# A graph layer on one core: 35 packed and 14 gathered blocks for 37 and 12, with evictions on either of two engines

## The chip, the cores and the metric

The kernel runs on one core of one Trainium2 chip. The metric is the device time of one execution in microseconds (us). Five engines take part: TensorE (PE in the profile), VectorE (DVE), ScalarE (ACT), GpSimd (POOL) and SyncE (SP, which only issues DMAs).

## The reference, cut to what matters

`x` holds 6250 rows of 128 numbers; 100,000 edges go from row `src` to row `dst`, sorted by `dst`, each of one of two types.

```python
Xs = X[src]
m_data = Xs @ W_data.T + b_data
m_ctrl = Xs @ W_control.T + b_control
msg = jnp.where((edge_types == 0)[:, None], m_data, m_ctrl)
agg = jax.ops.segment_sum(msg, dst, num_segments=X.shape[0])
out = jax.nn.relu(agg + (X @ W_self.T + b_self))
x = layernorm(x + out)          # over the last axis, eps 1e-5
```

So every row receives the sum of the messages of its incoming edges, adds its own product, passes through relu, is added to `x` and normalised.

## The kernel before, in words

**The table.** A message depends only on the source row and the type, so the kernel first computes all 2 x 6250 possible messages: per block of 128 rows one fp32 matmul with the two weights (`multiply`, L453). Each result is split into three bf16 pieces whose sum is the fp32 value (`take`, `leave`), which is why a message is 384 numbers wide. The table stays in SBUF as `m3` (98 tiles of 128 rows) and is also written to HBM (`store`).

**The destinations.** The 6250 rows are 49 blocks of 128. A block's edges lie in a window of 18 x 128 edges, found from the sorted list (`starts`). Blocks are summed in one of two ways.

*Packed blocks* (the first 37, NPB). They are prepared in groups (GROUPS, L36: eight groups of 4 or 5 blocks). For a group, `edge_fields` derives each edge's table tile and row; `bucket_hots` makes one-hot tables `hot_st` (L546); `ranks` numbers the edges of each table tile with a chain of 18 steps, each a matmul with `tri` on PE, a reduction `slot` on VectorE (L563) and a matmul with `rest` on PE; `fill_a` and `fill_b` (L600) place the edges in 32 slots per tile; `fill_c` writes the slots to HBM (`packed`) and treats those that did not fit. Then, per block, SP spreads 784 KB of slots over all partitions (`rows`, L718), VectorE makes one-hots of them (L725), and the block is done in 25 steps (NS). A step selects the messages of four table tiles with four column matmuls (`gather`, "g", L754) into one of four PSUM buffers, evicts them from PSUM to bf16 (`evict`, "e", L769) into one of eight SBUF buffers, and adds them to their destinations with four more (`add_up`, "s"). The helper `by_columns` (L232) issues these four matmuls, of 32 columns each; many different sums therefore show under L232.

*Gathered blocks* (the last 12, NG). GpSimd fetches the messages of 128 edges straight from the HBM table with an indirect DMA (`gather_rows`, "msg", L854), 18 for a block, into MB = 3 buffers. One-hots of the destinations (`gathered_hots`, L866) and four column matmuls each (`gathered_sums`, "gm") add them up.

Both kinds add the block's own product (`own_of`), sum the three pieces, apply relu, add `x` and take mean and variance on VectorE (`finish_blocks`, `finish_gathered`). `normalise` works on a group, or on the GQ blocks of a gathered piece, at a time: a root on ScalarE, a few small VectorE steps, one ScalarE `apply` per block (L190), one store.

**What sets the order.** Each engine executes its instructions in the order in which the program emits them, and waits where an operand is missing. That order is written by `Order.run` (L76): every stream above yields steps with a name, a cost per allowed engine ("T", "V", "A", "G", "S" for TensorE, VectorE, ScalarE, GpSimd, SP) and the steps that it needs. The planner keeps a clock per engine, takes the step that can start first, and among those that can start within 0.1 us on that engine the one that is due first. A step that may run on two engines goes to the one where it can start sooner, ScalarE at a tie. `due` (L388) computes the due times from constants: BUILT, when the table is complete; BLOCK, the time for a packed block; PACE, the time for one gathered tile, which is also the planned cost of a gather on GpSimd; AHEAD and FIRST, how long before its first block the preparation of a group has to end.

Before the change an eviction may go to VectorE only in the last group:

```python
costs = {"A": 0.37, "V": 0.53} if b >= STARTS[-1] else {"A": 0.37}
e = yield step(("e", b, g), costs, ("g", b, g), *free)
```

Of the kernel before, what the change touches and what calls it, by code (L numbers as in the profile page):

```python
# [32 lines left out]
ES = ER // RJ  # L33
EPS = 1e-05

GROUPS = (4,)*2+(5,)*5+(4,)  # L36
Q = max(GROUPS)
NPG = len(GROUPS)
NPB = sum(GROUPS)
NG = NB - NPB  # L40
STARTS = [sum(GROUPS[:i]) for i in range(NPG)]
R = 32
# [58 lines left out]
def step(name, costs, *needs, lag=0.0):  # L101
    return as_tuple(name), costs, [as_tuple(n) for n in needs], lag
# [7 lines left out]
def kernel(  # L110
# [95 lines left out]
    with ExitStack() as main:  # L206
        sums_over_windows(main, tc, x, xt, edges, w, bias, table, packed, total,
                          add_parts, finish, load_rows, norm)
# [6 lines left out]
def sums_over_windows(ctx, tc, x, xt, edges, w, bias, table, packed, total,  # L215
                      add_parts, finish, load_rows, norm):
    nc = tc.nc
    V, A, G, T = nc.vector, nc.scalar, nc.gpsimd, nc.tensor
# [64 lines left out]
    for j in range(RJ):  # L283
# [17 lines left out]
    counted = {n: const.tile([P, P, n], BF16, name=f"count{n}")  # L301
               for n in sorted({DC, CH, *GROUPS})}
    tri = const.tile([P, P], BF16, name="tri")
# [5 lines left out]
    slot_values = [const.tile([P, (Q + 1) // 2, NT], BF16, name=f"vs{i}") for i in range(2)]  # L309
    slot_b = {n: const.tile([P, R, n], BF16, name=f"slot{n}") for n in sorted({*GROUPS})}  # L310

# [68 lines left out]
                  for g, n in enumerate(PARTS) for b in range(at_part[g], at_part[g] + n, 2)]  # L380


    LEAD, BUILT = 8.0, 78
    BLOCK = 12.9
    PACE = 2.2
    AHEAD, FIRST = 22.0, 14

    def due(kind, *i):  # L388
        if kind in ("p", "g") and i[0] in ("root", "rooted", "scale", "apply", "out"):
            n = i[1] + 1  # L390
            return BUILT + 10 + (BLOCK * sum(p[2] for p in PIECES[:n]) if kind == "p" else PACE * KT * GQ * n)
        if kind in ("counted", "turned", "first"):
# [21 lines left out]
        if kind in ("win", "xs", "agg", "o", "whole", "sum"):  # L414
            b = i[0]
            begun = BUILT + (BLOCK * b if b < NPB else PACE * KT * (b - NPB))
            if kind == "win":
                return due("fields", blocks[b][0]) - 8 if b < NPB else BUILT - 20
            if b >= NPB:
                return begun + {"whole": PACE * KT + 2, "sum": PACE * KT + 5}.get(kind, 0)  # L420
            return begun + {"whole": BLOCK + 0.5, "sum": BLOCK + 3}.get(kind, 0.3 * BLOCK)
        if kind in ("rows", "sel", "d", "g", "e", "s"):
            of = {"rows": 1, "sel": 1, "d": 2}.get(kind, NS)
            lead = {"rows": -9, "sel": -3, "d": -1, "g": 0, "e": 1, "s": 2}[kind]
            return BUILT + BLOCK * (i[0] + (i[1] / of if len(i) > 1 else 0)) + lead
        if kind in ("gh", "gm", "msg"):
            k = i[1] * CH if kind == "gh" else i[1]
            return BUILT + PACE * (i[0] * KT + k) + {"msg": 0, "gh": 2, "gm": 5}[kind]
        n = GROUPS[i[0]]
        end = BUILT + BLOCK * STARTS[i[0]] - (AHEAD if i[0] else FIRST)  # L430
        span = BLOCK * n if i[0] else 34.0
        begun = end - span
# [324 lines left out]
    def evict():  # L757
        for i, (b, g) in enumerate(tiles):
            free = [("s", *tiles[i - EB])] if i >= EB else []
            if g == NS - 1 and b:  # L760
                free.append(("s", b - 1, g))
            costs = {"A": 0.37, "V": 0.53} if b >= STARTS[-1] else {"A": 0.37}
            e = yield step(("e", b, g), costs, ("g", b, g), *free)
            if g < NS - 1:
                gs, at = late.tile([P, D3], BF16, name="gs", bufs=EB), slice(P)
            else:
                gs, at = mixed[blocks[b][0] % 2], slice(2 * R, P)
            gs_tiles[b, g] = gs
            (A.copy if e == "A" else V.tensor_copy)(gs[at], g_tiles.pop((b, g))[at, :D3])  # L769
# [62 lines left out]
    rel_g = const.tile([P, NG, KT], BF16, name="rel_g")  # L832
    msgs, g_hots, kept = {}, {}, []
    GQ = -(-NG // -(-NG // Q))
    MB, XB = 3, 2

    def gathered_fields():
        yield step("idx", {"V": 1.8}, ("y", NB * 3 // 4), *[("win", b) for b in range(NPB, NB)])
# [10 lines left out]
    def gather_rows():  # L849
        for i, (j, k) in enumerate(gathered):  # L850
            free = [("gm", *gathered[i - MB])] if i >= MB else [*stored, "idx"]
            yield step(("msg", j, k), {"G": PACE}, *free, lag=3.0 - PACE)
            msgs[j, k] = late.tile([P, D3], BF16, name="msg", bufs=MB)
# [41 lines left out]
    def close_build():  # L895
# [7 lines left out]
        load_x(), starts(), edge_fields(), ranks(), fill_c(), fill_a(), fill_b(),  # L903
        spread(), select(), finish_blocks(),
        normalise([(lambda g=g: (hs_[g], mvs[g]), STARTS[g] + q0, q0, n) for g, q0, n in PIECES], "p"), add_up(), gather(), evict(), to_hots(), bucket_hots(),
        multiply(), take(0, "yh", "y"), leave(0, "y1", "yh"),
        take(1, "ym", "y1"), leave(1, "y2", "ym"), take(2, "yl", "y2"), constants(), store(), close_build(),
# [136 lines left out]
```

## Time and profile before

| | |
|---|---|
| time, median of 3 runs | 594.62 us (592.69 to 597.58) |
| profiled execution | 628.32 us |
| its span, first to last instruction | 626.6 us |
| mean granted TensorE clock | 0.978 |
| busy: PE, DVE, ACT, POOL | 554.5, 448.2, 448.4, 255.6 us |
| selections (L754) | 3626 matmuls |
| evictions (L769) | 892 on ACT, 33 on DVE |
| gathers (L854) | 216 |
| first selection; first and last packed sum (L153) | 82.4; 101.4 and 603.3 us |
| first gather issue; last gathered sum | 87.3; 609.5 us |

The profile is one execution, and the profiler makes it longer than an undisturbed one; the place of things is read from it, and the time from the runs. In the groups, `L754 PE MATMUL g_ps<-m,rows 128*32 128x384 bf16 x3626 | 347.7, 332 | 6.2 <-issue 2.9` means: line 754, on PE, 3626 matmuls that write `g_ps`; busy for 347.7 us in all where overlaps count once, 332 ns for one; PE had been idle for 6.2 us just before them, and most of that ended without a visible releaser. In the waits, a row names who waited, for whom, the total in us, how often, and the longest. A busy share of an engine is an average over stages, so the windows (busy time of each engine in one stretch) are read beside it.

### The profile page before, as it was taken

The numbers are of one execution on the slowest core, as the hardware profiler recorded it, in microseconds if no ns is written. First come the engines' busy times: TensorE is split into PE (matmuls) and PEld (weight loads), VectorE is DVE, ScalarE is ACT, GpSimd is POOL, SyncE is SP. The second block draws the span as 40 slices with busy tenths as digits, with TensorE's granted clock in tenths as the row PEclk, the third lists the DMA queues.
The fourth block names the chain that finished last, engine by engine and source line by source line (L and its number), as shares of the span: only waits on it lengthen the run. The fifth ranks groups of instructions, "written<-read, shape, count | busy, mean of one in ns | idle before, by whom it ended". The sixth has DMA issues, their size and how long they took to land.

```text
span 626.6 us, 27468 instructions
## 1 busy us (share of the span) xinstructions
PE 554.5 (88%) x11703; PEld 453.8 (72%) x11703; DVE 448.2 (72%) x1031; ACT 448.4 (72%) x1066; POOL 255.6 (41%) x232
## 2 busy tenths in 40 slices
PE   5899879999999989899999989999998899998950
PEld 3555447887887778787887877788886788777730
DVE  4645687897888786688768876788857766568650
ACT  6756546768877767688678768778787887777631
POOL 1000025544545445545455345455435444444330
PEclk9999989999999999999999999999999999999985
DMA  3669653243434442444324433434424443533120
GB/s 106 187 170 273 203 198 111 53 157 107 136 121 149 118 116 61 153 123 133 106 61 160 125 104 110 146 121 127 129 56 155 135 123 103 158 102 119 45 58 21
DMA packets 59642, 77.37 MB, mean 123 GB/s; under 512 B 15344, under 2 KB 50395, under 8 KB 59511
## 3 DMA queue, kind: packets, MB, share of 16 engines
q1 hardware_dynamic: 47653, 50.56, 25.4%
q0 software_dynamic: 10704, 21.56, 12.5%
q10 hardware_dynamic: 1154, 3.41, 1.8%
q8 instruction: 93, 1.52, 1.0%
q14 instruction: 38, 0.31, 0.2%
HBM read 62.44 MB, written 13.07 MB: 120 GB/s over the span
## 4 chain that ended last, share of the span: by engine, by line
PE 73%; DMA 9%; DVE 5%; issue 5%; ACT 4%; POOL 1%; SPq 1%; another core or an unknown queue 0%; ACTq 0%; POOLq 0%; DVEq 0%
PE agg L232 25%; PE g_ps L754 23%; PE acc L232 8%; DMA msg<-table,idx 7%; PE agg_g L232 6%; PE small L600 5%; PE y L460 3%; ACT gs L769 2%; PE y L478 1%; POOL msg L854 1%; DVE slot L563 1%; ACT h_p L190 1%; DMA rows<-packed 1%; PE y L462 1%; DVE two L584 1%
## 5 line engine op out<-in xcount | busy, mean ns | idle before, releaser
L769 ACT CAST gs<-g_ps 128x384 bf16<-128x384 f32 x856 | 357.8, 494 | 120.8 <-PE g_ps L754 85.7
L754 PE MATMUL g_ps<-m,rows 128*32 128x384 bf16 x3626 | 347.7, 332 | 6.2 <-issue 2.9
L854 POOL DMA_INDIRECT msg<-table,idx x216 | 243.4, 1127 | 263.6 <-PE agg_g L232 122.7
L232 PE MATMUL agg<-gs,hot_d 128*32 128x384 bf16 x3552 | 321.9, 334 | 16.7 <-ACT gs L769 8.2
L232 PEld LDWEIGHTS <-hot_d 128*32 128x32 bf16 x3700 | 212.5, 137 | 47.1 <-issue 36.3
L754 PEld LDWEIGHTS <-rows 128*32 128x32 bf16 x3626 | 201.4, 138 | 31.2 <-issue 25.6
L563 DVE TENSOR_REDUCE slot<-acc 128x5 bf16<-128x490 f32 (+1 forms) x144 | 90.2, 627 | 76.2 <-PE acc L232 49.8
L232 PE MATMUL agg_g<-msg,hot_g 128*32 128x384 bf16 x864 | 93.7, 333 | 13.5 <-DMA msg<-table,idx 11.2
L739 DVE TENSOR_TENSOR hot_d<-count,to 128x1664 bf16<-128x1664 bf16 x74 | 78.7, 1066 | 10.8 <-ACT to L634 5.1
L600 PE MATMUL small<-hot_st,two 128*32 128x98 bf16 x1332 | 66.2, 283 | 2.3 <-DVE ls L684 1.5
L232 PE MATMUL acc<-hot_st,tri 128*32 128x490 bf16 (+1 forms) x576 | 65.4, 359 | 0.2 <-issue 0.2
L232 PE MATMUL acc<-hot_st,rest 128*32 128x490 bf16 (+1 forms) x544 | 60.1, 361 | 6.2 <-DVE slot L563 5.6
L232 PEld LDWEIGHTS <-hot_g 128*32 128x32 bf16 x864 | 46.0, 124 | 19.5 <-issue 18.1
L471 ACT CAST m<-y 128x512 bf16<-128x512 f32 (+1 forms) x75 | 40.9, 580 | 25.9 <-PE y L462 12.8
L600 PEld LDWEIGHTS <-two 128*32 128x32 bf16 x1332 | 53.9, 116 | 6.5 <-issue 2.9
L546 DVE TENSOR_TENSOR hot_st<-count,st_b 128x2940 bf16<-128x2940 bf16 (+1 forms) x24 | 45.0, 1880 | 13.5 <-PE small L600 9.7
L694 POOL DMA_INDIRECT mixed<-table,row_i x8 | 9.9, 1234 | 83.2 <-DVE rows L725 79.0
L725 DVE TENSOR_SCALAR rows<-rows,pid 128x3136 bf16<-128x3136 bf16 x37 | 38.6, 1042 | 2.8 <-DMA rows<-packed 2.3
L460 PE MATMUL y<-w_sb,xt 128*128 128x256 f32 x98 | 34.4, 438 | 1.8 <-DMA xt<-in_xt 1.8
L232 PEld LDWEIGHTS <-rest 128*32 128x32 bf16 x544 | 24.1, 98 | 15.1 <-issue 14.3
L153 DVE TENSOR_REDUCE whole<-agg 128x128 f32<-128x384 f32 x37 | 20.5, 553 | 11.2 <-PE agg L232 5.6
L769 DVE CAST gs<-g_ps 128x384 bf16<-128x384 f32 x32 | 17.2, 555 | 15.2 <-PE g_ps L754 14.4
(140 smaller groups left out, 440.6 us busy)
## 6 DMA issues: line engine op xcount, KB each, us to landing
rows<-packed SPq DMA_DIRECT2D x37, 784.0 KB
table<-m SPq DMA_DIRECT2D x10, 768.0 KB
msg<-table,idx POOLq DMA_INDIRECT x216
xt<-in_xt ACTq DMA_DIRECT2D x5, 512.0 KB
xt_p<-in_xt SPq DMA_DIRECT2D x37, 64.0 KB
xs_p<-in_x SPq DMA_DIRECT2D x37, 64.0 KB
out<-h_p SPq DMA_DIRECT2D x5, 320.0 KB
win<-in_edges SPq DMA_DIRECT2D x37, 27.0 KB
```

The source lines that it names most:

```text
L153: nc.vector.tensor_reduce(whole, agg.rearrange("p (i c) -> p c i", i=3), axis=AX.X, op=ALU.add)
L232: T.matmul(out[c : c + 32], lhsT[:, c : c + 32], rhs, **flags)
L460: T.matmul(y[:, j, :], xts[g][:, b + j - at_part[g], :], w_sb[:, : 2 * D], start=j == 0, stop=False, skip_group_check=True)
L471: A.copy(part_of(b, n, i), ys[b][:, :n, :].rearrange("p b (t c) -> p t b c", t=2))
L546: V.tensor_tensor(hot, counted[n][:, None, 1 : NT + 1, :].to_broadcast([P, KC, NT, n]), fields[grp][2][:, c * KC : c * KC + KC, None, :].t ...
L563: V.tensor_reduce(slots[grp][:, k, :], by_q, axis=AX.X, op=ALU.max)
L600: T.matmul(vt[c0 : c0 + R, q // 2, :], two[:, k % KC, i, :, q], hot[:, k % KC, :, q], start=k == 0 and q < 2, stop=k == KT - 1, skip_group ...
L725: V.tensor_scalar(rows[b], rows[b], pid1, None, op0=ALU.is_equal)
L739: V.tensor_tensor(hot, counted[DC][:, :, :n], places[grp][:, q, None, c * DC : c * DC + n].to_broadcast([P, P, n]), op=ALU.is_equal)
L754: T.matmul(g_ps[t * R : (t + 1) * R, :D3], rows[b][:, :, s], m3[:, s, :], start=True, stop=True)
L769: (A.copy if e == "A" else V.tensor_copy)(gs[at], g_tiles.pop((b, g))[at, :D3])
L854: G.indirect_dma_start(out=msgs[j, k], out_offset=None, in_=table[:, :], in_offset=bass.IndirectOffsetOnAxis(ap=idx[:, j, k : k + 1], axis=0),
```

## The change

Seven groups of five blocks replace the eight groups, so 35 blocks are packed and 14 gathered. The condition on the eviction is dropped, so the planner may give any eviction to VectorE. The gathers get five buffers for three and a planned pace of 1.75 us for 2.2. The other constants of the due times move with these. GQ, the number of gathered blocks that are normalised together, follows from NG and Q and becomes 5 (pieces of 5, 5 and 4) where it was 4.

```diff
-GROUPS = (4,)*2+(5,)*5+(4,)
+GROUPS = (5,)*7
...
-    LEAD, BUILT = 8.0, 78
-    BLOCK = 12.9
-    PACE = 2.2
-    AHEAD, FIRST = 22.0, 14
+    LEAD, BUILT = 8.0, 76
+    BLOCK = 13.1
+    PACE = 1.75
+    AHEAD, FIRST = 26.0, 20
...
-            costs = {"A": 0.37, "V": 0.53} if b >= STARTS[-1] else {"A": 0.37}
+            costs = {"A": 0.37, "V": 0.53} 
...
-    MB, XB = 3, 2
+    MB, XB = 5, 2
```

## The prediction

> **What bounds the kernel now.** I read the page first for the engines' shares and the slices, then the windows for one stage at a time, the timeline for how closely TensorE issues, the waits for who is late, and the groups for durations.
>
> ```profile
> span 626.6 us, 27468 instructions
> PE 554.5 (88%) x11703; PEld 453.8 (72%) x11703; DVE 448.2 (72%) x1031; ACT 448.4 (72%) x1066; POOL 255.6 (41%) x232
> PE   5899879999999989899999989999998899998950
> ```
>
> TensorE (PE) is the busiest, with nines almost throughout; VectorE (DVE) and ScalarE (ACT) follow at 72% each. By the windows:
>
> ```profile
> core 0: us, PE busy (x) PEld busy (x) DVE busy (x) ACT busy (x) POOL busy (x), PEclk, DMA share, GB/s
> 300.00:350.00 50.00, 47.35 (x1120) 41.02 (x1114) 38.67 (x82) 36.82 (x91) 24.59 (x23) 1.00 0.40 123
> 500.00:550.00 50.00, 47.72 (x1129) 40.15 (x1121) 31.89 (x76) 39.38 (x97) 22.69 (x22) 1.00 0.42 128
> ```
>
> In the steady stage PE is busy 47 of 50 us, DVE 39, ACT 37. A busy PE need not be a full one, so I look at its spacing:
>
> ```profile
> 340.94 0.39 PE L754 MATMUL g_ps<-m,rows 128*32 128x384 bf16 x4
> 341.11 0.39 PE L232 MATMUL agg_g<-msg,hot_g 128*32 128x384 bf16 x4
> 341.27 0.39 PE L232 MATMUL agg<-gs,hot_d 128*32 128x384 bf16 x4
> ```
>
> Four column matmuls start every 0.164 us although one lasts 0.33: when nothing is late, the four-matmul set is the unit of work and costs 0.164 us. The waits say how much of that is lost:
>
> ```profile
> POOL msg L854 <- PE agg_g L232: 122.7, 78, 3.8
> POOL msg L854 <- PE g_ps L754: 107.0, 96, 4.1
> ACT gs L769 <- PE g_ps L754: 85.7, 126, 7.1
> DVE slot L563 <- PE acc L232: 49.8, 43, 2.4
> PE agg_g L232 <- DMA msg<-table,idx: 11.2, 10, 2.4
> PE agg L232 <- ACT gs L769: 8.2, 15, 1.1
> ```
>
> Everybody waits for PE, hundreds of microseconds in total; PE waits for others only some tens. POOL's gathers wait for PE to free one of three buffers. So a PE instruction taken out of the steady stage should shorten it.
>
> [...] The trace has 555 and 494, and 0.51 and 0.42 apart when queued. [...] the chain shows [...] 7.71 for one that shares the engines with a 784 KB spread of rows.
>
> ```profile
> L769 ACT CAST gs<-g_ps 128x384 bf16<-128x384 f32 x856 | 357.8, 494 | 120.8 <-PE g_ps L754 85.7
> L754 PE MATMUL g_ps<-m,rows 128*32 128x384 bf16 x3626 | 347.7, 332 | 6.2 <-issue 2.9
> L854 POOL DMA_INDIRECT msg<-table,idx x216 | 243.4, 1127 | 263.6 <-PE agg_g L232 122.7
> L769 DVE CAST gs<-g_ps 128x384 bf16<-128x384 f32 x32 | 17.2, 555 | 15.2 <-PE g_ps L754 14.4
> ```
>
> **The change, part by part.** The sum is against the profiled execution, 628.3 us (span 626.6 and 1.7 around it); the median of the runs shown is 594.62, 0.946 of it, and I scale the result with that.
>
> (a) *Blocks 36 and 37 turn from packed to gathered.* PE time of a packed block: selection 98 matmuls / 4 x 0.164 = 4.02; adding 25 x 0.164 = 4.10; ranks, 35 sets per group of five at about 0.21 = 7.35 / 5 = 1.47; filling, 36 matmuls of 98 columns at 0.055 (the chain takes 0.11 for two) = 1.98; own rows 0.28; positions and list about 0.3. Sum 12.1. A gathered block: 18 x 0.164 + 0.28 = 3.2. Check: 37 x 12.1 + 12 x 3.2 = 486, less the ranking and filling of the first eight blocks (8 x 3.45 = 28, done before the first selection) = 458, in the 521 us from the first selection (82.4) to the last packed sum (603.3): 88% of the stage, consistent with windows of 47 in 50 that also hold latencies. Two blocks: 2 x 8.9 = 17.8 us of PE work; at the same 88%, **-20.2**. It all lies on the bound; bounds -17.8 (the lost 12% doesn't shrink) and -24.
>
> (b) *36 more gathers*, each one POOL issue of 1.13 us: 41 us, POOL from 41% to about 50% busy. Covered by POOL's 264 us of waiting. DVE gets two blocks of hot_g (3 x 0.55) and loses two blocks of packed work (about 10.8 from 38.6/50 x 13.94 us per block); SP loses two spreads, two loads and two pairs of own-row loads, and gets as many for the gathered list. 0 on the path.
>
> (c) *Pace 1.75 and five buffers.* Today the gathers run from 87.3 to 606.2, 2.41 us each. The due times put the last gathered matmuls at 76 + 441 + 5 = 522 in planned time, packed blocks end at 76 + 13.1 x 35 = 534.5; today it is 558 against 555. In the trace the gathered end is indeed late: last packed sum 603.3, last gathered 609.5, and four `apply` steps and a store after it.
>
> ```profile
> 609.53 0.56 DVE L153 TENSOR_REDUCE whole<-agg_g 128x128 f32<-128x384 f32 x1 [3.19 <-PE agg_g L232]
> 612.66 1.65 ACT L190 ACTIVATE h_g<-h_g,shift,rstd 128x128 f32<-128x128 f32 x4 [1.25 <-DVE shift L184]
> ```
>
> With packed blocks last, the end is the one-block piece, whose apply ended at 606.9 today, against 614.3: at most -7.4; I take **-5**, least 0 if gathers stay last. Of the 11.2 us for which PE waits for gathers, 3.8 lie in that end; a buffer's round of 5 x 1.9 against 3 x 2.4 us leaves room for the 7.71 us landing: **-3**, bounds -7 and +8 [...].
>
> (d) *Seven groups of five; FIRST, BUILT, BLOCK, AHEAD.* The first group grows by a block: DVE slot 18 x (0.664 - 0.565) = 1.8, hot_st 3 x 0.31 = 0.9, hr and two 3 x 0.3 = 0.9, before the first selection; one constant copy (0.5 on ACT) goes. **+3**, bounds 0 and +6. The four-wide tables go elsewhere at no cost. GQ goes from 4 to 5: three normalisations of gathered blocks as before. Due times only reorder.
>
> (e) *Evictions on either engine.* How many move? In the last group, where both may do it now, DVE took 33 of 100; there DVE's other work fills 17.6 of 50 us (33.7 less 16.05 of evictions), 65% free. In the steady stage 23% is free. In proportion 33% x 23/65 = 12%, **2.9 of 25 per block**; this is my estimate, bounds 0 and 6. Thirty blocks make 87, the last five 40, less 33 today: 94 more x 0.555 = +52 us on DVE, -46 on ACT. DVE in the steady stage goes from 77% to 88%. What I add is a queueing cost: DVE works in order, and an eviction may sit behind a 2 us hot_st or a slot that waits for PE, with PE's adding matmul waiting for it. If one in four holds PE for 0.25 us: 87 x 0.25 x 0.25 = **+5**; the gain from a less crowded ACT, out of the 8.2 + 2.6 us that PE waits for it, I put at 0 net of that. Bounds -8 and +25.
>
> Sum: -20.2 - 5 - 3 + 3 + 5 = **-20**: 608 profiled, x 0.946 = **576**. What is late next is DVE, not ACT.
>
> **Rivals.**
> *DVE becomes the bound (slower).* Place: the steady stage, where DVE must keep the ranks of the next group, the one-hot tables and now evictions in one order. For: DVE is already at 77% and its longest operation is 2 us. Per packed block DVE has 10.75, with the larger gathered share (0.40 for 0.32 of 2.96 us) 10.98. At k evictions it is 10.98 + 0.555 k; if DVE can be filled to 93%, 35 blocks take as long as today's 516 us at k = 4.9. From five of 25 it decides; at k = 6, 35 x 14.3 / 0.93 = 538, +22: 650 profiled, **615**. Against: the planner gives VectorE an eviction only where it is free sooner. Chance 0.20, the milder part of it above 600.
> *The gathers don't reach the pace (no change).* 252 gathers in today's 519 us need 2.07 us each; POOL alone could do 1.13 + 0.3, buffers at worst (0.95 + 7.7 + 0.4) / 5 = 1.8. If landing times stretch with density and PE stalls on them, the gain of (a) is eaten: about **593**. Chance 0.16. Against: POOL waits for PE, not the reverse.
> *ACT was holding PE more than the waits show (larger gain).* PE fills the stage to 91%: 440 / 0.91 = 484, -37 with the same end and start: **557**. Chance 0.12.
> *No eviction moves.* The closer pace and two blocks remain, without the +5: 571; part of the forecast's case.
>
> **Numbers.** Forecast (567 to 586) 0.52, larger gain 0.12, no change 0.16, slower 0.20. Range 558 to 604: it leaves out the lower part of the larger gain (0.05) and most of the slow case's upper end (0.13). The runs before spread over 0.8%, so 1% is about what can be told from no change. Faster by over 1%: 0.66; within 1%: 0.14; slower: 0.20.
>
> **What would show it.** Per packed block the distance from first to last packed sum, divided by 34, stays near 13.9 us; selections fall from 3626 to 3430 and gathers rise to 252. (c) the last gathered sum comes before the last packed sum. (e) some 130 evictions on DVE, DVE at 85 to 90% in the steady windows and PE still at 94%. It is wrong if PE's waits for DVE evictions grow to tens of microseconds or PE falls under 45 in 50 (DVE rival), or if waits for gathers grow past 20 us (pace rival).

## The result and the profile after

The changed kernel takes 549.8 us (median of 4 runs, 548.52 to 551.42) where the kernel before takes 593.65 us beside it (590.95 to 597.58): ratio 0.926, 95% interval 0.920 to 0.932. Forecast were 576 us and a range of 558 to 604, so the sign was right and the gain was more than twice the forecast: 44 us where some 19 were expected.

One thing about the profile on which the prediction stood: that execution took 628.3 us, over 5% longer than every other execution of the same kernel in that set. A second profile of the kernel before took 602.4 us (span 600.7), and after is compared with that one from here on. That the profiler as such lengthens an execution, as I had written, isn't borne out: the profiled execution of the kernel after took 550.7 us, in the middle of its four runs, and of the eleven changed versions below it was the longest run in four and the shortest in three. The first lines of the page, of the kernel after:

```profile
span 549.0 us, 26381 instructions
PE 506.4 (92%) x11222; PEld 439.9 (80%) x11222; DVE 456.9 (83%) x1027; ACT 402.5 (73%) x943; POOL 294.6 (54%) x267
PE   5899978899999999999989999989999999989991
```

and of the kernel before, profiled again:

```profile
span 600.7 us, 27468 instructions
PE 533.0 (89%) x11703; PEld 459.9 (77%) x11703; DVE 446.4 (74%) x1031; ACT 445.0 (74%) x1066; POOL 256.4 (43%) x232
PE   5899968999998998899998989979997999989950
```

PE has less to do and is idle for less of the time; VectorE and GpSimd are busier. The windows of the kernel after (columns: stretch, its length, then busy time and instruction count of PE, weight loads, DVE, ACT, POOL, granted clock, DMA share, GB/s):

```profile
300.00:350.00 50.00, 49.60 (x1205) 45.03 (x1201) 45.40 (x95) 40.25 (x99) 35.01 (x31) 1.00 0.50 148
400.00:450.00 50.00, 49.45 (x1219) 45.32 (x1216) 45.32 (x107) 40.86 (x102) 34.61 (x30) 1.00 0.52 160
```

VectorE now works 45 of 50 us, as (e) foresaw, and PE is at 49.5 all the same. The groups of the kernel after that answer to those shown of before:

```profile
L769 ACT CAST gs<-g_ps 128x384 bf16<-128x384 f32 x739 | 313.5, 491 | 92.8 <-PE g_ps L754 72.5
L854 POOL DMA_INDIRECT msg<-table,idx x252 | 284.7, 1130 | 140.3 <-PE g_ps L754 70.9
L754 PE MATMUL g_ps<-m,rows 128*32 128x384 bf16 x3430 | 315.4, 331 | 0.1
L769 DVE CAST gs<-g_ps 128x384 bf16<-128x384 f32 x101 | 54.6, 553 | 19.2 <-PE g_ps L754 14.8
```

103 evictions went to VectorE (two more write `mixed`). Where the time went, by stage, from the second profile of before to the one of after:

| | before again | after | difference |
|---|---|---|---|
| start to first selection (L754) | 81.7 | 81.4 | -0.3 |
| first selection to last packed sum (L153) | 495.6 | 456.4 | -39.2 |
| last packed sum to the end of the span | 23.4 | 11.2 | -12.2 |
| span | 600.7 | 549.0 | -51.7 |

(The two profiled executions are 52 us apart, the medians 44.) The waits of the two point to the cause of much of it; the experiments below test it. Before, profiled again (who waited, for whom: total, times, longest):

```profile
POOL msg L854 <- PE agg_g L232: 104.8, 89, 4.2
POOL msg L854 <- PE g_ps L754: 91.7, 79, 4.4
PE agg_g L232 <- DMA msg<-table,idx: 31.0, 23, 3.3
```

After:

```profile
POOL msg L854 <- PE g_ps L754: 70.9, 124, 3.5
POOL msg L854 <- PE agg_g L232: 48.7, 68, 2.8
PE agg_g L232 <- DMA msg<-table,idx: 10.8, 9, 2.0
```

So POOL waited for PE, and PE waited for what POOL had issued too late. Such a circle through a set of buffers is called a ring here, and in the chain of waits of the kernel before (start, length, what) one of its turns looks like this:

```profile
314.24 1.38 POOL msg L854
315.62 0.39 issue
...
316.23 8.28 DMA msg<-table,idx
324.51 0.04 issue
324.56 0.46 PE agg_g L232 x4
325.02 0.32 PE agg L232 x4
325.34 0.32 PE g_ps L754 x4
```

From the moment when a buffer is free until its next content is in place there pass 1.4 + 0.4 + 8.3 us and small gaps, over 10 us. Three buffers at 2.3 us a gather give about 7.

### The profile page after: what moved, and what is told of

It is laid out like the page before. It is cut to its first block, busy times and chain, and to the rows that moved or that the text cites. A ratio compares the mean times of both kernels' runs of the same rounds, so it can differ in the third digit from the quotient of the medians.

```text
span 549.0 us, 26381 instructions
## 1 busy us (share of the span) xinstructions
PE 506.4 (92%) x11222; PEld 439.9 (80%) x11222; DVE 456.9 (83%) x1027; ACT 402.5 (73%) x943; POOL 294.6 (54%) x267
## 4 chain that ended last, share of the span: by engine, by line
PE 63%; DMA 15%; DVE 11%; ACT 4%; issue 3%; POOL 1%; SPq 1%; DVEq 0%; ACTq 0%; POOLq 0%
PE agg L232 20%; PE g_ps L754 19%; DMA msg<-table,idx 8%; PE acc L232 7%; PE small L600 6%; PE agg_g L232 6%; DMA rows<-packed 3%; PE y L460 3%; ACT gs L769 2%; DVE hot_st L546 2%; DVE slot L563 2%; ACT h_p L190 1%; DMA xt_p<-in_xt 1%; PE y L478 1%; POOL msg L854 1%
## 5 line engine op out<-in xcount | busy, mean ns | idle before, releaser
L769 ACT CAST gs<-g_ps 128x384 bf16<-128x384 f32 x739 | 313.5, 491 | 92.8 <-PE g_ps L754 72.5
L854 POOL DMA_INDIRECT msg<-table,idx x252 | 284.7, 1130 | 140.3 <-PE g_ps L754 70.9
L754 PE MATMUL g_ps<-m,rows 128*32 128x384 bf16 x3430 | 315.4, 331 | 0.1
L232 PE MATMUL agg<-gs,hot_d 128*32 128x384 bf16 x3360 | 295.3, 330 | 3.8 <-DVE gs L769 1.9
L754 PEld LDWEIGHTS <-rows 128*32 128x32 bf16 x3430 | 183.6, 136 | 16.8 <-issue 10.4
L232 PEld LDWEIGHTS <-hot_d 128*32 128x32 bf16 x3500 | 184.1, 137 | 13.9 <-issue 8.9
L232 PE MATMUL agg_g<-msg,hot_g 128*32 128x384 bf16 x1008 | 106.8, 329 | 10.9 <-DMA msg<-table,idx 10.8
L563 DVE TENSOR_REDUCE slot<-acc 128x5 bf16<-128x490 f32 x126 | 83.4, 662 | 19.6 <-PE acc L232 16.5
L769 DVE CAST gs<-g_ps 128x384 bf16<-128x384 f32 x101 | 54.6, 553 | 19.2 <-PE g_ps L754 14.8
L232 PEld LDWEIGHTS <-hot_g 128*32 128x32 bf16 x1008 | 51.7, 124 | 15.1 <-issue 13.5
L232 PE MATMUL acc<-hot_st,tri 128*32 128x490 bf16 x504 | 60.0, 374 | 1.2 <-DVE hot_st L546 1.2
L232 PE MATMUL acc<-hot_st,rest 128*32 128x490 bf16 x476 | 54.2, 376 | 7.4 <-DVE slot L563 7.0
L546 DVE TENSOR_TENSOR hot_st<-count,st_b 128x2940 bf16<-128x2940 bf16 x21 | 41.7, 1991 | 3.7 <-PE small L600 2.0
L232 PEld LDWEIGHTS <-rest 128*32 128x32 bf16 x476 | 21.0, 97 | 17.4 <-issue 16.2
L232 PEld LDWEIGHTS <-tri 128*32 128x32 bf16 x504 | 21.2, 98 | 3.3 <-issue 3.0
```

The lines of the kernel that those rows point to most:

```text
L232: T.matmul(out[c : c + 32], lhsT[:, c : c + 32], rhs, **flags)
L546: V.tensor_tensor(hot, counted[n][:, None, 1 : NT + 1, :].to_broadcast([P, KC, NT, n]), fields[grp][2][:, c * KC : c * KC + KC, None, :].t ...
L563: V.tensor_reduce(slots[grp][:, k, :], by_q, axis=AX.X, op=ALU.max)
L754: T.matmul(g_ps[t * R : (t + 1) * R, :D3], rows[b][:, :, s], m3[:, s, :], start=True, stop=True)
L854: G.indirect_dma_start(out=msgs[j, k], out_offset=None, in_=table[:, :], in_offset=bass.IndirectOffsetOnAxis(ap=idx[:, j, k : k + 1], axis=0),
```

## The experiments

Three theories were tried against each other. A: ScalarE's evictions held PE, and the freedom to use VectorE is the unforeseen gain. B: the blocks, the pace and the earlier end of the gathers are the gain. C: the ring of three buffers held PE, and five buffers are most of it.

**The kernel before, once more**, without an edit:

> The kernel before once more, for a second profile. The prediction took the 521 us from first selection to last packed sum as normal and read 88% of PE work in it. If that one execution was long by chance (628 us against 595), this one shows a stage of about 488 us and PE filled to about 94%, and then the cost of a block off PE weighs as predicted and the surplus of the change lies elsewhere. If it again shows 521 us for the stage, the profiler lengthens this kernel and not the changed one.

602.38 us in one execution, stage 495.6 us, shown above. So the 521 us belonged to that one execution. With the prediction's own 458 us of PE work the stage was filled to 92%, closer to the first case (94%) than to the 88% of the prediction.

**Evictions alone.**

```diff
-            costs = {"A": 0.37, "V": 0.53} if b >= STARTS[-1] else {"A": 0.37}
+            costs = {"A": 0.37, "V": 0.53}
```

> The kernel before with evictions allowed on either engine in all groups and nothing else. Theory A (ScalarE's evictions held PE; the freedom is the unforeseen gain): 570 or less. Theory B (the gain comes from the blocks, the pace and the end; the freedom is neutral): 588 to 597. The rival of the prediction (VectorE becomes the bound): above 600.

586.68 us, ratio 0.981 (0.973 to 0.989). A small gain, just under what B allows, and not the rival's loss; PE waits 22.0 us for gathers in its profile where it waited 31.0.

**The changed kernel with evictions as before** (the same line the other way round in the kernel after):

> The changed kernel with evictions on VectorE in the last group only, as before. Theory A: 570 to 580, the 25 us beyond the prediction are gone. Theory B: 548 to 556.

551.69 us, ratio to the kernel before 0.925 (0.918 to 0.933), where the change as a whole has 0.926. Theory A falls: within the changed kernel the freedom of the evictions brings nothing that can be measured. The 12 us that it brought in the kernel before (586.68 against 598.43) go with 9 us less waiting for gathers; what caused them wasn't tested.

**The changed kernel with three buffers.**

```diff
-    MB, XB = 5, 2
+    MB, XB = 3, 2
```

> The changed kernel with three buffers for the gathers in place of five. If the buffers carry the closer pace: a round of 3 x 1.75 = 5.3 us is shorter than issue and landing at their longest (0.95 + 7.7), PE waits for gathers by tens of us, and the time is 565 to 590. If the planned pace alone does it: within 3 us of 550.

608.48 us, ratio 1.018 (1.010 to 1.026): not the middling loss that I had written down, but slower than the kernel before. Without the two more buffers nothing is left of the gain. Its waits and the chain's shares:

```profile
PE agg_g L232 <- DMA msg<-table,idx: 52.5, 49, 3.9
DMA msg<-table,idx 34%; PE agg L232 13%; PE g_ps L754 12%; PE agg_g L232 5%; PE acc L232 5%; PE small L600 5%; POOL msg L854 3%; PE y L460 2%; ACT gs L769 1%; DMA rows<-packed 1%; DVE hot_st L546 1%; PE y L478 1%; ACT h_p L190 1%; DVE slot L563 1%; PE y L462 0%
```

In a third of the span the chain of waits runs through gathers in flight.

**Five buffers alone**, in the kernel before:

```diff
-    MB, XB = 3, 2
+    MB, XB = 5, 2
```

> The kernel before with five buffers for the gathers in place of three, nothing else. Theory C (the round of three buffers made PE wait in its order for gathers, and this is most of the surplus): the rows in which PE waits for gathers fall from 31 us to under 10, and the time to 560 to 572; the blocks then bring the other 10 to 20. Theory D (buffers matter only for the closer pace): within 4 us of the kernel before, 590 to 598.

564.37 us, ratio 0.955 (0.946 to 0.964): theory C: by the ratio 27 us (29 by the medians) of the 44, and with the old groups, the old pace and the old evictions. PE's wait for gathers fell from 31.0 to 3.4 us.

**The blocks alone**, with their pace and due times, but three buffers and evictions as before:

```diff
-GROUPS = (4,)*2+(5,)*5+(4,)
+GROUPS = (5,)*7
...
-    PACE = 2.2
+    PACE = 1.75
...
```

> The kernel before with the seven groups, the pace of 1.75 and the other due times, but three buffers and evictions on VectorE in the last group only. Prediction's step (a) (PE work is what counts): 573 to 582. Theory C: 36 more gathers through three buffers cost more than two packed blocks bring: 600 to 612, near the changed kernel with three buffers.

599.06 us over 20 runs, ratio 1.011 (1.008 to 1.015): a little slower, though just short of the loss that theory C had named. PE waits 45.0 us for gathers and 32% of the chain is gathers in flight. The two packed blocks are gone from PE here too; it doesn't show. This version and the changed kernel with evictions as before (551.69 us) differ in the number of buffers and in nothing else, so that two more buffers are worth 47 us here.

MB does two things: it sets how many tiles there are in memory, and the planner uses it for the order. **The order of three with five tiles in memory** has the same instructions in the same order on every engine as the kernel before (in the two traces DVE, ACT and POOL show the same sequence, 1031, 1066 and 232 instructions, one by one; on PE matmuls that overlap can't all be told apart in order):

```diff
-            msgs[j, k] = late.tile([P, D3], BF16, name="msg", bufs=MB)
+            msgs[j, k] = late.tile([P, D3], BF16, name="msg", bufs=5)
```

> The kernel before with its own order of instructions on every engine, planned for three buffers, but five buffers in memory. Theory C1 (the round of the buffers at run time is what held PE): 562 to 570, as with five buffers in plan and memory. Theory C2 (the plan for five buffers places the gathered matmuls better): 585 to 597.

568.88 us, ratio 0.961 (0.954 to 0.967): theory C1.

**The order of five with three tiles:**

```diff
-    MB, XB = 3, 2
+    MB, XB = 5, 2
...
-            msgs[j, k] = late.tile([P, D3], BF16, name="msg", bufs=MB)
+            msgs[j, k] = late.tile([P, D3], BF16, name="msg", bufs=3)
```

> The order that is planned for five buffers, with three in memory, nothing else changed from the kernel before. C1: 590 to 615, gathers held back by the buffers. C2: 562 to 572.

603.98 us, ratio 1.016 (1.008 to 1.025). With the order unchanged, the tiles in memory alone are worth 24 us in the one order and some 40 us in the other (603.98 against the 564.37 above). It is the ring at run time. (That the order of five brings some microseconds more than that of three, 0.955 against 0.961, isn't shown: the intervals overlap.) The waits of the order of three with five tiles:

```profile
POOL msg L854 <- PE agg_g L232: 80.7, 72, 3.0
POOL msg L854 <- PE g_ps L754: 73.8, 97, 3.3
PE agg_g L232 <- DMA msg<-table,idx: 3.5, 5, 1.6
```

POOL still waits 155 us for PE in these two rows, and now it is harmless: with two more tiles ahead, what it issues is early enough.

**Eight buffers in the changed kernel** (`MB, XB = 8, 2`):

> The changed kernel with eight buffers in place of five. If five still let PE wait (10.8 us in its trace): 540 to 547. If five cover every landing that can be covered, and the rest is PE work: within 3 us of 550.

544.82 us, ratio to the kernel before 0.923 (0.915 to 0.932); PE's wait for gathers is 4.1 us for 10.8. The time is 5 us under that of the change, but the two weren't run side by side and the intervals of their ratios overlap, so that five buffers left something open is likely and not shown.

**More gathered blocks.** Sixteen, six buffers, in the changed kernel:

```diff
-GROUPS = (5,)*7
+GROUPS = (5,)*6+(3,)
...
-    BLOCK = 13.1
+    BLOCK = 13.3
-    PACE = 1.75
+    PACE = 1.55
...
-    MB, XB = 5, 2
+    MB, XB = 6, 2
```

> Changed kernel carried on: groups of 5 x 6 and 3, so 33 packed and 16 gathered blocks, pace 1.55, BLOCK 13.3, six buffers. If PE work alone decides, two more blocks bring 17.8 us again: 530 to 536. If POOL's issue (1.13 us and a 0.3 us gap, 288 gathers, 412 us) or landing comes near the pace: 545 to 560.

546.8 us, ratio 0.929 (0.919 to 0.938), the second case. The last packed sum comes at 520.3, the last gathered one at 531.5: the gathers end last again.

**Sixteen, ten buffers, pace 1.45** (the same edit with `PACE = 1.45`, `MB, XB = 10, 2`):

> The sixteen gathered blocks once more, with ten buffers and a pace of 1.45, close to what POOL's issue alone allows (1.13 + 0.3). If the sixteen blocks lost to the gathers' late end before: 530 to 540. If POOL and the landings can't go faster: 544 to 552.

554.07 us, ratio 0.934 (0.927 to 0.941): both of my cases are missed. The late end is gone (the last gathered sum comes at 526.5, the last packed one at 538.5), and yet nothing is gained; that it is 7 us slower than with pace 1.55 isn't shown, since the two weren't run side by side and the intervals overlap. Its waits:

```profile
POOL msg L854 <- PE g_ps L754: 38.4, 126, 0.3
PE agg_g L232 <- DMA msg<-table,idx: 23.1, 24, 2.4
```

POOL never waits longer than 0.3 us, so it is issuing without a pause, at (518.4 - 94.0) / 287 = 1.48 us a gather, while PE waits 23.1 us for gathers: as I read it, an issuer that never pauses has no time to fill ten buffers. That this is why the ten buffers brought nothing is argued from these lines; a slower pace with ten buffers wasn't tried.

**Fifteen, eight buffers, pace 1.6:**

```diff
-GROUPS = (5,)*7
+GROUPS = (5,)*6+(4,)
...
-    BLOCK = 13.1
+    BLOCK = 13.2
-    PACE = 1.75
+    PACE = 1.6
...
-    MB, XB = 5, 2
+    MB, XB = 8, 2
```

> Changed kernel with eight buffers, groups of 5 x 6 and 4 (34 packed, 15 gathered), pace 1.6, BLOCK 13.2. If PE work still decides: one block brings 8.9 us off 544.8, 535 to 539. If the gathers end last again: 543 to 548.

540.5 us (538.15 to 542.3), ratio to the kernel before 0.913 (0.906 to 0.919), between my two cases. It beats both kernels (the change has 0.926, 0.920 to 0.932), with eight buffers and one block more at once. The last gathered sum (518.5) is 6 us ahead of the last packed one (524.5). Against the eight-buffer run the one block makes 4 us by the medians, half of the price of PE work, but the two weren't run side by side either and their intervals overlap: what the block alone brings isn't shown.

## Why the prediction was wrong, point by point

**The step that failed is the reading "Everybody waits for PE".** I took POOL's 230 us of waiting for PE (the two rows shown) as evidence that the gathers can't be the limit ("POOL waits for PE, not the reverse"), and PE's own wait for gathers at the 11.2 us of that one execution. Both rows belong to one ring: PE frees a buffer, POOL issues, the transfer lands, PE goes on. Then each side waits for the other, and the larger total only says which side has more slack. The chain of waits shows a ring better. Its shares in the second profile of the kernel before:

```profile
PE agg L232 20%; PE g_ps L754 18%; DMA msg<-table,idx 17%; PE acc L232 8%; PE agg_g L232 5%; PE small L600 4%; PE y L460 3%; POOL msg L854 3%; DMA rows<-packed 2%; PE y L478 1%; ACT h_p L190 1%; ACT gs L769 1%; PE y L462 1%; SPq L368 1%; DVE hot_st L546 1%
```

That is 17% for gathers in flight and 3% for their issue. The first profile, the only one that I had, shows 7% and 1%, no more for the gathers in flight than the kernel after (8%), so there the chain could raise the question and not settle it. The sum that settles it was in the prediction: (c) sets a round of 3 x 2.4 = 7.2 us beside a landing of 7.71 and still gives it 3 us, and in the second rival I wrote (0.95 + 7.7 + 0.4) / 5 = 1.8 us a gather for five buffers. For the three of the kernel before, the same sum is 3.0 us, above its real pace of 2.3 to 2.4: a gather at its longest had to hold PE.

**(c) was mis-sized for that reason.** The -3 for five buffers is -24 in the order of before and, by the ratio, -27 with the order replanned, where the bounds were -7 and +8, the +8 an estimate with no trace behind it. The other half of (c) had the mechanism right: the gathers end before the packed blocks (last gathered sum 533.8, last packed 537.8), and the end shrank by 12 us where I took 5 and allowed 7.4. What I left out is the stretch from the issue of the last store to the end of the span: 12.2 us in the second profile of before, where the last gathered blocks go out last, and 7.6 after, where a single block does. That the smaller store is the reason wasn't tested.

**(a) was right in kind and too high.** With five buffers and the old evictions, the new groups and pace take 564.37 to 551.69, 13 us by the medians (18 by the ratios; the two weren't run side by side). Their profiles: the stage falls by 12.4 us (464.4 to 452.0), the end by 7.5, the first selection comes 4.5 later. I had priced 20.2 for the stage. With five buffers, the 458 us of PE work that I added up fill 464.4 us, 99%. The sum is some 7 us low, since not all ranking and filling of the first eight blocks lies ahead of the first selection, as I assumed: the trace has 204 of their 280 matmuls for ranks there and 192 of 288 for filling. At my prices that makes an estimated 465 us, all of the stage, so the prices are about right and leave no room for a latency. What goes with the missing part of (a) is that PE waits 6.7 us for gathers instead of 3.4 and 11.3 for ranks (`slot`) instead of 5.3; that these waits are the whole of it is argued.

**The fill of 88%** that I carried over unchanged was thus no property of the kernel's work. It was partly that one long execution, partly the ring. The long execution's stage is 25 us above the second's although PE waits 20 us less for gathers in it; PE's busy time is 21 us longer (554.5 against 533.0), and the weight loads of L232 and L754 are idle for 98 us in place of 69. I have no cause for it.

**(d)** +3 for the first group of five: the change starts its first selection 0.3 us earlier than before, the version without free evictions 3.1 us later. The first is just outside the bounds of 0 and 6. Among all the versions this start scatters between 80.3 and 84.8 us, so neither figure tells much.

**(e)** 127 evictions were expected on VectorE, 103 came; VectorE at 91% of the steady windows for 88%. The queueing cost isn't there: in the kernel after, PE's addings wait 1.9 us for VectorE's evictions in all. So the rival that VectorE becomes the bound is refuted at this share, and the rival that ScalarE had been holding PE is refuted as the source of the gain, by 551.69 against 549.8. That rival's 557 us (559 by its own terms) came nearest to the measured time, for a reason that doesn't hold: that is luck. "No eviction moves" would have given the same time. (Queued evictions start 0.47 us apart on VectorE and 0.37 on ScalarE, by the median of the first profile, where I read 0.51 and 0.42; no term of the sum rests on it.)

**(b)** The gathers' issue on POOL was indeed hidden, but not their landing: PE waited 31.0 us for gathers before, profiled again, and 10.8 after.

**The scale** of 0.946 from the long profiled execution to the median turned -20 into -19 and did no harm to speak of; the stage lengths it came from did.

## What to carry to other kernels

Where two engines wait for each other through a set of buffers, don't weigh the two rows against each other: add up one round (free, issue, landing, use) at its longest and divide it by the number of buffers, and compare that with the pace that the consumer needs. Here it was 3.0 us against 2.4, and two more tiles of 98 KB were worth 24 to 27 of the 44 us, more than the rest of the change. Look at that before work is moved off the engine that looks full: with three buffers, the same two blocks and their pace made the kernel a little slower (ratio 1.011). As argued above, and not tested, more buffers can't help an issuer that has no time to fill them: where POOL issued without a pause, at 1.48 us a gather, ten left PE waiting 23.1 us.

## What the runs showed that I had not expected

A stall of PE can cost more than its length. In the kernel before (profiled again), PE waits 2.20 us for the gather whose landing took 8.28, and for the next 3.4 us its four-matmul sets start 0.32 us apart where they start 0.16 apart otherwise:

```profile
321.98 0.37 PE L754 MATMUL g_ps<-m,rows 128*32 128x384 bf16 x4
324.56 0.46 PE L232 MATMUL agg_g<-msg,hot_g 128*32 128x384 bf16 x4 [2.20 <-DMA msg<-table,idx]
324.72 0.62 PE L232 MATMUL agg<-gs,hot_d 128*32 128x384 bf16 x4
325.02 0.64 PE L754 MATMUL g_ps<-m,rows 128*32 128x384 bf16 x4
325.34 0.64 PE L232 MATMUL agg<-gs,hot_d 128*32 128x384 bf16 x4
...
327.90 0.51 PE L754 MATMUL g_ps<-m,rows 128*32 128x384 bf16 x4
328.18 0.38 PE L232 MATMUL agg<-gs,hot_d 128*32 128x384 bf16 x4
328.35 0.38 PE L754 MATMUL g_ps<-m,rows 128*32 128x384 bf16 x4
```

The windows show the clock that was granted there, 0.59 of full speed in the mean of four microseconds:

```profile
320.00:324.00 4.00, 2.35 (x60) 2.06 (x58) 3.83 (x12) 2.14 (x5) 2.68 (x2) 1.00 0.69 251
324.00:328.00 4.00, 3.44 (x47) 2.97 (x50) 1.50 (x3) 1.76 (x4) 1.03 (x1) 0.59 0.14 38
328.00:332.00 4.00, 4.00 (x100) 3.85 (x96) 2.78 (x4) 3.44 (x9) 2.41 (x3) 0.98 0.09 25
```

The slow stretch came right after the 2.20 us without matmuls and lasted some 3.4 us; over the next four microseconds the granted clock was 0.98. What lowers the clock wasn't tested. Some 11 sets at 0.32 instead of 0.164 us are 1.7 us on top of the 2.2.

Not every stall was followed by one. Of the eight stalls of 1.5 us or more in this profile between 100 us and the last packed sum, the four of 2.20 to 3.26 us were followed by such a stretch (granted clock 0.57 to 0.60 over the next four microseconds), the four of 1.50 to 2.02 us were not (1.00). Nor does the length alone tell them apart: in the first profile of the kernel before a stall of 2.36 us, which ended at 235.26, was followed by a clock of 1.00 over four microseconds. The account comes out roughly: between this profile and that of the order of three with five tiles PE's wait for gathers falls by 27.5 us, four slow stretches, at the 1.7 us of this one, are an estimated 6.8, together 34.3, and the spans differ by 34.9 (600.7 and 565.8).

It fits that the mean granted clock is 0.961 to 0.973 in the profiles in which PE waits 22 us or more for gathers (before again, evictions alone, the three others with three buffers, sixteen with ten buffers) and 0.976 to 0.990 in those with 16 us or less. That mean also takes in the end of the span, where PE has next to nothing to do (0.57 over the last 23 us of the kernel before, profiled again), so it is a rough measure.
